# A transformer block on one core: early sums moved to GpSimd, loads and turnings placed anew, the last output behind the loop over other pairs

## The chip, the core and the metric

The kernel runs on one core of a Trainium2 chip. The core has TensorE (PE, matrix products into PSUM; its weight loads are listed apart as PEld), VectorE (DVE), ScalarE (ACT), GpSimd (POOL) and SyncE (SP). SP and ACT issue most of the DMAs, POOL the indirect ones. The metric is the time on the device in microseconds, of one execution of the whole program; lower is better.

## The reference

The input is x: 8 sequences of 512 rows of 256 numbers, all in fp32.

```
x = x + layernorm(attention(layernorm(x)))
x = x + layernorm(ffn(layernorm(x)))
```

The attention has 16 query heads of width 128 in 4 groups that share keys and values, a causal mask, biases and a sinusoidal position term added to queries and keys; an output product brings 2048 back to 256. The ffn routes each of the 4096 rows to 6 of 64 experts by a softmax. Each expert takes the first 64 rows that chose it, in row order, and no more: `d = (silu(rows @ w_gate) * (rows @ w_up)) @ w_down`, weighted by the score of the row. To their sum a shared expert of inner width 352 is added for every row.

## The kernel before, in words

The order of all instructions on the five engines is written out by hand: inside `tc.manual_schedule` each engine runs what the Python code records, in the order in which it records it. So the place of a call in the code is its place in each engine's queue, DMAs included.

The main loop (L998) runs over k = 0 to 127, one attention head of one sequence per round (b = k // 16, s = k % 16). A round is called a head, or a slot, below. Per head: `scores` (four triangular tiles psc, reduced on DVE to e and least, exponentiated on ACT), `weigh` (four scalings of e, on POOL, for the last head on DVE), `turned` (DVE transposes e in 32x32 blocks to eb, SP stores it to DRAM as ex_d and reads it back in turn as et), `mix` (et times values into pav, evicted by ACT as ao), `project` (ao times the output weights into po), `queries` (pq, evicted by DVE as qt). These belong to different heads: while head k is scored, head k - 1 is turned, k - 2 mixed, k - 3 projected. The last two heads are turned on TensorE instead (`turned_at_once`, L373), with evictions of the four tiles pe alternating between ACT and DVE.

Between these stand side tasks at named places of a head: A and B after `weigh` and `project`, M after `queries`, D at the end. They are the preparation of the next sequence (`prepare`: load of x, statistics, keys and values) and the feed-forward part of the previous one (`feed_forward`: residual sum, normalised rows xg, shared expert with products psg and psu, routing). For the first four sequences the turned rows xt go through DRAM too, as exr_d: four writes at the step "6M", and a read behind the next head's writes of ex_d.

The experts are served in two ways. After five sequences (EARLY = 5) the experts are computed in pairs of two, 32 pairs, by the generator `experts` (L662), advanced two or four times per head from head 94 on. One pair in its turn: `start_pair` gathers rows by an indirect DMA on POOL (gx), `turn_rows` turns them on TensorE (ptx, copied by DVE to gxt), `gate_up`, `gate_up_hidden`, `turn_hidden` (pth, ht), `down` (pd, dd), `scatter` (an indirect adding DMA to y_d). Weights are loaded on ACT's queue. An iteration of the generator has two halves. When all pairs are done, `finish_early` (L969) adds the two halves of y_d for the first five sequences, normalises and stores the output: one sequence starts every four half slots, each with `finish` (L699), which takes seven of them.

The last three sequences are served for one pair "late", which still has places free, with products inside `feed_forward` and `last_part` (L886). Further such pairs, if any, are served by a loop over other pairs (L1073), whose count is computed at run time. In the profiled execution no instruction of the loop's body is listed: the count is zero. `last_part` works through the feed-forward of sequence 7, with the shared expert and the output of sequence 6 in between.

PSUM pools ps_s (scores, turnings) and ps_m (products) have three buffers each. Before the first experts run, `zeros` (L228) clears the second half of y_d by 21 stores on SP; the main loop advances it twice per head in the first sequence.

## Time and profile before

| what | us |
|---|---|
| runs: median (lowest, highest) | 1431.27 (1430.13, 1436.82) |
| the profiled execution's own time | 1429.28 |
| its span, from the first to the last instruction | 1427.6 |
| TensorE busy | 1383.4 (97%) |
| VectorE, ScalarE, GpSimd busy | 895.4, 500.2, 433.7 |
| mean granted TensorE clock | 0.994 |
| DMA moved | 262.5 MB, mean 184 GB/s |

A row of the profile names a line of the kernel, an engine, an operation and the tiles that it writes and reads ("psc<-kt,qt"). Times are in microseconds unless marked ns. A wait names the instruction that ended it. "PEclk" is the share of TensorE's full clock that the chip granted. An engine that stands costs time only if the end of the program hangs on it.

### The profile page before, as it was taken

Reading aid. Unit: us, or ns where it says so; the run is one execution under the profiler, and the core shown is the slowest. Engines: PE = TensorE matmul, PEld = TensorE weight load, DVE = VectorE, ACT = ScalarE, POOL = GpSimd, SP = SyncE. Lnnn points to the kernel's source line nnn. Section 1 sums busy time; section 2 is a strip of 40 time slices with the busy share of each in tenths; the row PEclk is TensorE's granted clock in tenths of the full one; section 3 lists DMA queues with packets and bytes.
Section 4 is the critical chain, followed back from the end, with each engine's and each line's share of the span. In section 5 each row is a group of like instructions: output and inputs, shape, how many; then the busy total and the mean of one; then the engine's idle time right before and its main releaser. Section 6 shows DMA issues by size and latency. Waiting matters only on the chain.

```text
span 1427.6 us, 18526 instructions
## 1 busy us (share of the span) xinstructions
PE 1383.4 (97%) x5230; PEld 841.4 (59%) x5230; DVE 895.4 (63%) x3127; ACT 500.2 (35%) x1432; POOL 433.7 (30%) x698
## 2 busy tenths in 40 slices
PE   9999999999999999999999999999989999999895
PEld 5665665666556665656556665655546565556463
DVE  5565577656775577557765677566656545677634
ACT  2332344224332334234422433233433333444421
POOL 2222242213321242114221232124545344444311
PEclk9999999999999999999999999999999999999998
DMA  7774566546763576455654566459999889877702
GB/s 243 204 225 146 140 181 198 146 119 171 215 177 107 150 208 193 110 140 164 207 164 125 155 173 193 107 147 276 302 246 258 225 239 252 210 236 250 240 30 82
DMA packets 167990, 262.50 MB, mean 184 GB/s; under 512 B 17212, under 2 KB 142109, under 8 KB 167885
## 3 DMA queue, kind: packets, MB, share of 16 engines
q1 hardware_dynamic: 133069, 212.00, 50.5%
q10 hardware_dynamic: 28672, 39.85, 9.4%
q0 software_dynamic: 6144, 9.44, 3.4%
q8 instruction: 42, 0.69, 0.2%
q14 instruction: 63, 0.52, 0.1%
HBM read 148.25 MB, written 112.99 MB: 183 GB/s over the span
## 4 chain that ended last, share of the span: by engine, by line
PE 80%; DMA 7%; DVE 7%; issue 2%; ACT 2%; POOL 1%; SPq 1%; ACTq 0%; DVEq 0%; POOLq 0%
PE pav L390 16%; PE psc L328 15%; PE pq L315 13%; PE po L402 13%; PE pk L285 4%; PE pv L296 4%; PE psg L749 3%; PE psu L749 3%; PE pgu L590 2%; PE py L776 2%; PE pd L616 2%; DMA wd<-in_w_down 2%; DVE eb L361 1%; DMA exr_d<-xb_f 1%; ACT e L335 1%
## 5 line engine op out<-in xcount | busy, mean ns | idle before, releaser
L345 POOL TENSOR_SCALAR e<-e,recip 128x128 f32<-128x128 f32 x508 | 268.5, 574 | 757.6 <-DVE recip L342 744.0
L335 ACT ACTIVATE e<-e,least 128x128 f32<-128x128 f32 (+3 forms) x512 | 285.8, 559 | 349.2 <-DVE least L332 337.1
L328 PE MATMUL psc<-kt,qt 128*128 128x128 f32 (+3 forms) x1024 | 306.3, 438 | 8.6 <-DVE least L332 6.0
L390 PE MATMUL pav<-et,v 128*128 128x512 f32 (+3 forms) x1024 | 297.5, 434 | 3.3 <-DMA et<-ex_d 3.0
L390 PEld LDWEIGHTS pav<-et,v 128*128 128x128 f32 x1024 | 194.1, 190 | 165.7 <-issue 116.8
L332 DVE CUSTOM_DVE_ANT_0 e<-psc,mask 128x128 f32<-128x128 f32 (+3 forms) x512 | 232.6, 479 | 56.3 <-PE psc L328 49.4
L402 PE MATMUL po<-wo_sb,ao 128*128 128x256 f32 x1024 | 243.5, 381 | 0.7 <-ACT ao L110 0.7
L315 PE MATMUL pq<-xnt,wq_sb 128*128 128x512 f32 x512 | 242.2, 596 | 0.0
L402 PEld LDWEIGHTS po<-wo_sb,ao 128*128 128x128 f32 x1024 | 193.1, 190 | 72.0 <-issue 41.0
L110 ACT COPY ao<-pav 128x512 f32<-128x512 f32 x128 | 74.9, 585 | 443.8 <-PE pav L390 429.6
L361 DVE STREAM_TRANSPOSE eb<-e 128x128 f32<-128x128 f32 x756 | 227.4, 364 | 3.5 <-DMA ex_d<-eb 3.2
L328 PEld LDWEIGHTS psc<-kt,qt 128*128 128x128 f32 x1024 | 164.6, 191 | 76.7 <-DVE least L332 26.9
L318 DVE SCALAR_TENSOR_TENSOR qt<-pq,bq_sb,pe_sb 128x512 f32<-128x512 f32 x128 | 95.6, 747 | 104.6 <-PE pq L315 104.4
L315 PEld LDWEIGHTS pq<-xnt,wq_sb 128*128 128x128 f32 x512 | 96.3, 191 | 69.7 <-issue 64.3
L342 DVE RECIPROCAL recip<-total 128x4 f32<-128x4 f32 x128 | 22.8, 178 | 120.2 <-ACT e L335 120.2
L335 ACT ACTIVATION_READ_ACCUMULATOR e<-e,least 128x1 f32 x512 | 95.8, 187 | 0.0
L627 POOL DMA_INDIRECT y_d<-dd,idx x32 | 50.9, 1591 | 102.0 <-DMA y_d<-dd,idx 51.5
L285 PE MATMUL pk<-xnt,wkv_sb 128*128 128x512 f32 x128 | 59.3, 594 | 0.2 <-ACT xnt L110 0.2
L296 PE MATMUL pv<-wkv_sb,xnt 128*128 128x512 f32 x128 | 58.1, 593 | 0.0
L298 DVE TENSOR_TENSOR v<-pv,bv_sb 128x512 f32<-128x512 f32 x32 | 22.1, 691 | 49.7 <-PE pv L296 49.7
L288 DVE SCALAR_TENSOR_TENSOR kt<-pk,bk_sb,pe_sb 128x512 f32<-128x512 f32 x32 | 24.0, 750 | 44.1 <-PE pk L285 44.1
L113 DVE COPY ht<-pth 88x256 f32<-88x256 f32 x32 | 13.4, 418 | 56.6 <-PE pth L607 56.6
(200 smaller groups left out, 1100.0 us busy)
## 6 DMA issues: line engine op xcount, KB each, us to landing
ex_d<-eb SPq DMA_DIRECT2D x504, 160.0 KB
et<-ex_d SPq DMA_DIRECT2D x126, 640.0 KB
wgu<-in_w_gate ACTq DMA_DIRECT2D x32, 352.0 KB
wgu<-in_w_up ACTq DMA_DIRECT2D x32, 352.0 KB
wd<-in_w_down ACTq DMA_DIRECT2D x32, 352.0 KB
y<-y_d ACTq DMA_DIRECT2D x10, 512.0 KB
x<-in_x SPq DMA_DIRECT2D x8, 512.0 KB
x_d<-x SPq DMA_DIRECT2D x8, 512.0 KB
```

The costliest lines, as they stand in the source:

```text
L285: nc.tensor.matmul(pk, lhsT=wkv_sb[:, c, g, 0, :], rhs=s["xnt"][:, c, :], start=c == 0, stop=c == NC - 1)
L296: nc.tensor.matmul(pv, lhsT=s["xnt"][:, c, ts(i, P)], rhs=wkv_sb[:, c, :, 1, :], start=c == 0, stop=c == NC - 1)
L315: nc.tensor.matmul(pq, lhsT=wq_sb[h // QPG][:, c, ts(h % QPG, D)], rhs=seqs[b]["xnt"][:, c, :], start=c == 0, stop=c == NC - 1)
L318: nc.vector.scalar_tensor_tensor(qt, pq, bq_sb[:, h : h + 1], pe_sb, ALU.add, ALU.add)
L328: nc.tensor.matmul(psc[:, :w], lhsT=l["qt"][:, ts(i, P)], rhs=seqs[b]["kt"][h // QPG][:, :w], start=True, stop=True)
L332: nc.vector.tensor_tensor_reduce(out=e, in0=psc[:, :w], in1=mask[:, T - w :], scale=-1.0 / math.sqrt(D), scalar=BIG, op0=ALU.add, op1=ALU. ...
L335: nc.scalar.activation(e, e, AF.Exp, bias=l["least"][:, i : i + 1], scale=-1.0, accum_out=l["total"][:, i : i + 1])
L345: engine.tensor_scalar(e, e, recip[:, n : n + 1], 1.0, ALU.mult, ALU.mult)
L361: nc.vector.transpose(blocks.rearrange("p c j t -> p j c t"), l["e"][i][:, js[0] * P : (js[-1] + 1) * P].rearrange("p (j c t) -> p j c t", ...
L390: nc.tensor.matmul(pav[:, :, j:, :], lhsT=seqs[b]["v"][:, j, ts(g, D)], rhs=l["et"][:, :, AT[j] : AT[j] + NI - j, :], start=j == 0, stop=j ...
L402: nc.tensor.matmul(po[b][i // 2][:, i % 2, :], lhsT=ao[:, ts(i, P)], rhs=wo_sb[:, h, :], start=h == 0 and i % 2 == 0, stop=h == NH - 1, sk ...
L749: nc.tensor.matmul(as_taken(pp[:mw, :], xt2), lhsT=w_sb[:, c, ds(f0, mw)], rhs=in_order(xt2, c), start=c == 0, stop=c == NC - 1)
```

## The change

- `zeros` is advanced once per head, in heads 0 to 22, instead of twice per head in heads 0 to 15.
- The load of the next sequence's x (the first step of `prepare`, at s = 6) is issued after step M instead of ahead of `queries`.
- `turn_rows` moves from the first half of an iteration of `experts` to the end of the second half.
- The down weights of the late pair are loaded in head 104 instead of 102.
- `finish`: the sum of the two halves is made by GpSimd, one half slot later, with the load of x1 beside it and a half slot of nothing behind it; a sequence takes nine half slots, and the steps end two half slots later.
- `output`: shift is computed in two parts, a product with -1 on DVE and a product with rs on GpSimd, both ahead of the pause.
- The last two heads: the project of head 124 goes ahead of the turning of head 126, whose evictions all go to DVE; the eviction of the last pav is split between DVE and ACT.
- `last_part` no longer stores x1 and y of sequence 7, gives sequence 6's output earlier places, and ends with the late pair's dd. The rest, `last_output`, comes after the loop over other pairs. In the loop, sequence 7 adds its term directly to the sums in PSUM.

```diff
--- before.py
+++ after.py
@@ -370,7 +370,7 @@
             l["et"] = p2.tile([P, NI, NB, BS], F32, tag="et", name=f"et_{k}")
             nc.sync.dma_start(out=l["et"].rearrange("s a n t -> s (a n t)"), in_=ex.rearrange("p a f -> p (a f)"))
-        def turned_at_once(k):
+        def turned_at_once(k, evictions=(on_act, on_dve) * 2):
             l = live[k]
             l["et"] = p2.tile([P, NI, NB, BS], F32, tag="et", name=f"et_{k}")
@@ -378,8 +378,8 @@
                 pt = ps_s.tile([P, NI, NI, BS], F32, tag="s", name=f"pe_{k}_{j}")
                 for i in range(j, NI):
                     nc.tensor.transpose(pt[:, i - j, :, :].rearrange("p a t -> p (a t)"), l["e"][i][:, ts(j, P)], ident)
-                (on_act, on_dve)[j % 2](l["et"][:, :, AT[j] : AT[j] + NI - j, :].rearrange("p a n t -> p n a t"),
-                                        pt[:, : NI - j, :, :])
+                evictions[j](l["et"][:, :, AT[j] : AT[j] + NI - j, :].rearrange("p a n t -> p n a t"),
+                             pt[:, : NI - j, :, :])
         def mix(k):
             b, h = divmod(k, NH)
@@ -390,7 +390,12 @@
                 nc.tensor.matmul(pav[:, :, j:, :], lhsT=seqs[b]["v"][:, j, ts(g, D)],
                                  rhs=l["et"][:, :, AT[j] : AT[j] + NI - j, :], start=j == 0, stop=j == NI - 1)
             l["ao"] = p2.tile([D, T], F32, tag="ao", name=f"ao_{k}")
-            on_act(l["ao"].rearrange("d (i a t) -> d i a t", i=NI, a=NI), pav.rearrange("d a i t -> d i a t"))
+            ao, rows = l["ao"].rearrange("d (i a t) -> d i a t", i=NI, a=NI), pav.rearrange("d a i t -> d i a t")
+            if k < NK - 1:
+                on_act(ao, rows)
+            else:
+                on_dve(ao[:, :2], rows[:, :2])
+                on_act(ao[:, 2:], rows[:, 2:])
         def project(k):
             b, h = divmod(k, NH)
@@ -668,8 +673,7 @@
             for m in range(NM + 5):
                 if m < NM:
                     start_pair(m)
-                for behind_, step in ((5, down), (3, gate_up), (4, turn_hidden), (2, turn_rows),
-                                      (1, load_gate_up), (3, load_down)):
+                for behind_, step in ((5, down), (3, gate_up), (4, turn_hidden), (1, load_gate_up), (3, load_down)):
                     if 0 <= m - behind_ < NM:
                         step(m - behind_)
                 yield
@@ -677,6 +681,8 @@
                     gate_up_hidden(m - 3)
                 if 0 <= m - 5 < NM:
                     scatter(m - 5)
+                if 0 <= m - 2 < NM:
+                    turn_rows(m - 2)
                 if m >= 2:
                     next(later, None)
                 if m == NM + 4:
@@ -686,8 +692,10 @@
         def output(b, y, x1):
             mv, rs = norm_scales(tiles_of(y), f"y{b}")
-            yield
-            shift = shifts(mv, rs, f"y{b}")
+            shift = small.tile([P, NI], F32, tag="shift", name=f"shift_y{b}")
+            nc.vector.tensor_scalar_mul(shift, mv[:, :, 0], -1.0)
+            nc.gpsimd.tensor_tensor(shift, shift, rs, ALU.mult)
+            yield
             for i in range(NI):
                 scale_on_act(y[:, i, :], y[:, i, :], rs, shift, i)
             for i in range(NI):
@@ -702,9 +710,11 @@
             for k in range(2):
                 nc.scalar.dma_start(out=ys[k], in_=rows_of(y_d, k * (ET_ROWS + CAP) + b * T))
             yield
+            yield
+            yield
             x1 = residual(b, *tags[2])
-            yield
-            nc.vector.tensor_add(ys[0], ys[0], ys[1])
+            nc.gpsimd.tensor_add(ys[0], ys[0], ys[1])
+            yield
             yield
             for n, _ in enumerate(output(b, ys[0], x1)):
                 yield
@@ -918,7 +928,6 @@
             transpose_rows(xt2, xg, f"f{b}")
             for i in range(NI):
                 nc.gpsimd.tensor_scalar(xt[:, i, :], xt[:, i, :], shift[:, i : i + 1], 1.0, ALU.add, ALU.mult)
-            nc.sync.dma_start(out=rows_of(x1_d, b * T), in_=xt)
             other["part"](py6, 0)
             f = shared(b, xt2, l, "msmsms")
             next(f)
@@ -937,32 +946,33 @@
             gather("late", [(xg, marked[0])])
             gt = turn_scores(marked[1], b, p2, "kt", 5)
             gate_up("late")
-            next(f)
+            output6()
             py = l["py"] = [ps_o.tile([P, 2, E], F32, tag=f"o{n}", name=f"py_{b}_{n}") for n in range(2)]
             l["part"](py, 2)
             l["part"](py, 1)
             gate_up_hidden("late")
+            next(f)
+            output6()
             turn_hidden("late")
             l["part"](py, 0)
+            output6()
             down("late")
-            output6()
-            output6()
-            output6()
-            for i in range(NI):
-                nc.tensor.matmul(py[i // 2][:, i % 2, :], lhsT=gt[:, ts(i, P)], rhs=pairs["late"]["dd"],
-                                 start=False, stop=True, skip_group_check=True)
+            return py, xt, gt, pairs["late"]["dd"]
+
+        def last_output(py, x1, gt, dd):
+            b = B - 1
+            for i in range(NI):
+                nc.tensor.matmul(py[i // 2][:, i % 2, :], lhsT=gt[:, ts(i, P)], rhs=dd, start=False, stop=True,
+                                 skip_group_check=True)
             mv, rs = norm_scales([py[i // 2][:, i % 2, :] for i in range(NI)], f"y{b}")
             y = p2.tile([P, NI, E], F32, tag="xnt", name=f"y_{b}")
-            for n in range(2):
-                nc.scalar.copy(y[:, ts(n, 2), :], py[n])
-            nc.sync.dma_start(out=rows_of(ly_d, b * T - ET_ROWS), in_=y)
-            for i in range(NI):
-                nc.vector.tensor_scalar(o[:, i, :], py[i // 2][:, i % 2, :], mv[:, i, 0:1], None, ALU.subtract)
-            for i in range(NI):
-                nc.vector.scalar_tensor_tensor(xt[:, i, :], o[:, i, :], rs[:, i : i + 1], xt[:, i, :],
-                                               ALU.mult, ALU.add)
+            for i in range(NI):
+                nc.vector.tensor_scalar(y[:, i, :], py[i // 2][:, i % 2, :], mv[:, i, 0:1], None, ALU.subtract)
+            for i in range(NI):
+                nc.vector.scalar_tensor_tensor(x1[:, i, :], y[:, i, :], rs[:, i : i + 1], x1[:, i, :], ALU.mult, ALU.add)
                 if i % 2:
-                    nc.sync.dma_start(out=rows_of(out, b * T)[:, i - 1 : i + 1, :], in_=xt[:, i - 1 : i + 1, :])
+                    nc.sync.dma_start(out=rows_of(out, b * T)[:, i - 1 : i + 1, :], in_=x1[:, i - 1 : i + 1, :])
+
         EARLY_TAGS = [(p3, "wgu"), (p3, "wd")]
@@ -970,9 +980,9 @@
             rows = [finish(b, EARLY_TAGS + [[(p1, "xn"), (p2, "xnt")][b % 2]]) for b in range(EARLY)]
             yield
-            for t in range(4 * EARLY + 3):
+            for t in range(4 * EARLY + 5):
                 for b in range(EARLY):
-                    if 0 <= t - 4 * b < 7:
+                    if 0 <= t - 4 * b < 9:
                         next(rows[b])
                 yield
@@ -1007,32 +1017,32 @@
             scores(k, 2)
             scores(k, 3)
             if k == NK - 1:
-                turned_at_once(k - 1)
+                project(k - 3)
+                turned_at_once(k - 1, (on_dve,) * NI)
             weigh(k)
             side(s, "A")
-            if k >= 3:
+            if 3 <= k < NK - 1:
                 project(k - 3)
             side(s, "B")
             if active and not finishing:
                 next(routed, None)
             if s == 9 and b <= EARLY + 1:
                 next(ahead)()
-            if s == 6 and b <= EARLY:
-                ahead = prepare(b + 1)
-                next(ahead)()
             if k + 1 < NK:
                 queries(k + 1)
             if finishing:
                 next(routed, None)
             side(s, "M")
+            if s == 6 and b <= EARLY:
+                ahead = prepare(b + 1)
+                next(ahead)()
             if b <= EARLY and s == 8:
                 next(ahead)()
             if k >= 2:
                 mix(k - 2)
             if active and not finishing:
                 next(routed, None)
-            if not b:
-                next(zeroing, None)
+            if k < NH + 7:
                 next(zeroing, None)
             if k == FIRST_FREE:
@@ -1042,6 +1052,7 @@
                 pairs["late"] = {"m": table["m"], "wgu_at": {"tag": "wgu_late", "bufs": 1},
                                  "wd_at": {"tag": "wd_late", "bufs": 1}}
                 load_gate_up("late")
+            if k == FIRST_FREE + 2:
                 load_down("late")
             if s == 2 and b:
                 behind = feed_forward(b - 1)
@@ -1065,7 +1076,7 @@
         turned_at_once(NK - 1)
         mix(NK - 1)
         project(NK - 1)
-        last_part(behind, routed)
+        sums, *last = last_part(behind, routed)
         order.close()
@@ -1080,7 +1091,7 @@
                 q, tag = [(p1, "hid"), (p2, "v"), (p2, "v")][b - EARLY]
                 xg = q.tile([P, NI, LROW], F32, tag=tag, name=f"rest_xg_{b}")
                 nc.sync.dma_start(out=xg, in_=rows_of(lxg_d, b * T - ET_ROWS))
-                q, tag = [(p1, "y"), (p2, "x"), (p2, "x")][b - EARLY]
+                q, tag = [(p1, "y"), (p2, "x"), (p1, "xt2")][b - EARLY]
                 mark, marked = marks(m, xg[:, :, E:ROW], xg[:, :, ROW:], f"rest_{b}", q, tag)
                 parts.append((xg, mark))
                 gts.append(turn_scores(marked, f"rest_{b}", p2, "kt", 5))
@@ -1089,7 +1100,10 @@
             gate_up_hidden("late")
             turn_hidden("late")
             down("late")
-            for b in range(EARLY, B):
+            for i in range(NI):
+                nc.tensor.matmul(sums[i // 2][:, i % 2, :], lhsT=gts[-1][:, ts(i, P)], rhs=pairs["late"]["dd"],
+                                 start=False, stop=False, skip_group_check=True)
+            for b in range(EARLY, B - 1):
                 y = p2.tile([P, NI, E], F32, tag="xnt", name=f"rest_y_{b}")
                 nc.sync.dma_start(out=y, in_=rows_of(ly_d, b * T - ET_ROWS))
                 for i in range(NI):
@@ -1099,6 +1113,8 @@
                 nc.sync.dma_start(out=rows_of(ly_d, b * T - ET_ROWS), in_=y)
                 for _ in output(b, y, residual(b, p1, "xn")):
                     pass
+        with tc.manual_schedule(engines={ET.PE, ET.DVE, ET.Activation, ET.Pool, ET.SP}):
+            last_output(sums, *last)
 # ---- launch: one core ----
```

## The prediction

> **What bounds the kernel now.** I read the page first, for the engine that is never free; then the waits of that engine; then the stages where it waits.
>
> ```profile
> PE 1383.4 (97%) x5230; PEld 841.4 (59%) x5230; DVE 895.4 (63%) x3127; ACT 500.2 (35%) x1432; POOL 433.7 (30%) x698
> ```
>
> TensorE is busy for 1383.4 of 1427.6 us, and the change takes no TensorE instruction from the work. It can win only among the 44.2 us in which TensorE stands: 15.4 after its last matmul (1412.2), 1.9 ahead of its first, and some 27 of waits. Its waits by releaser:
>
> ```profile
> PE psc L328 <- DVE least L332: 6.0, 6, 2.4
> PE psg L749 <- DMA xt<-exr_d: 4.7, 4, 1.5
> PE pav L390 <- DMA et<-ex_d: 3.0, 3, 2.3
> PE pd L616 <- DMA wd<-in_w_down: 2.9, 2, 2.1
> PE ptx L579 <- DMA gx<-xg_d,idx: 2.3, 1, 2.3
> PE pe L380 <- ACT et L110: 2.2, 1, 2.2
> ```
>
> Total, times, longest: no wait repeats in every head; each is one collision at one place, and nearly each of these places is touched by the change. Two of them cost more than they say. TensorE by time around the first turning of gathered rows (start, duration, in brackets the standing before):
>
> ```profile
> 964.88 0.48 PE L579 MATMUL ptx<-ident,gx 128*128 128x128 f32 x2 [2.27 <-DMA gx<-xg_d,idx]
> 965.19 3.25 PE L315 MATMUL pq<-xnt,wq_sb 128*128 128x512 f32 x4
> ```
>
> The stretches of 10 us around it and around the wait for wd (length; busy time of PE, PEld, DVE, ACT, POOL; granted clock; DMA share; GB/s):
>
> ```profile
> 960.00:970.00 10.00, 7.73 (x21) 4.02 (x20) 4.83 (x19) 2.31 (x8) 4.98 (x7) 0.83 0.95 330
> 970.00:980.00 10.00, 10.00 (x50) 5.80 (x49) 5.79 (x24) 4.51 (x13) 1.31 (x3) 1.00 0.77 224
> ...
> 1050.00:1060.00 10.00, 7.63 (x31) 3.94 (x29) 5.01 (x18) 3.85 (x15) 1.50 (x2) 0.83 0.98 270
> ```
>
> After the 2.27 us of standing the clock is 0.83 and four query matmuls take 3.25 us, elsewhere 1.88.
>
> **Early stage: zero stores and the x load.** One store of zeros a head instead of two, over 22 heads instead of 11. The row is the wait for et (2.3 at 109.9 us, 0.25 at 86): its read was issued at 106.3 behind two stores of 128 KB and landed about 112.6. One of them gone, at some 200 GB/s, is 0.65 us, and 0.5 of SP issue; the same holds for the head before. I take 2.0 of 2.55 (0 to 2.5). The longer tail of stores ends in head 21, ahead of the exchange in head 22.
>
> The x load of the next sequence moves behind step M, so behind the four exchange writes on SP:
>
> ```profile
> 215.07 0.40 SPq L167 DMA_DIRECT2D x<-in_x  x1
> 215.56 2.48 SPq L133 DMA_DIRECT2D exr_d<-xb_f  x4
> 218.09 2.80 SPq L366 DMA_DIRECT2D ex_d<-eb  x4
> 222.13 0.34 SPq L135 DMA_DIRECT2D xt<-exr_d  x1
> ```
>
> The read at 222.13 waited for the writes, which ran behind 512 KB of x, and the last ex_d write waited for the x load's landing (220.59). Without both the read goes out 1 to 2 us earlier, and each of the four psg waits is 0.9 to 1.5 us: 3.5 of 4.7 (0 to 4.7). What is late instead is x, which is not read until the next head.
>
> **Expert stage.** Turning the gathered rows moves half an iteration later, past the step M or D and POOL's scatter. The first wait, 2.3 us, falls away: the rows came at 964.9, and the new place, behind the mix, is about 968. [...]
>
> The turning also held PSUM: psc's second tile waited for the copy of ht in the buffer before it, 0.2 us (start to start 0.33 where 0.11 is usual, at 1124.24) in 15 of these heads. In the changed order two score tiles and the turning lie apart: 15 x 0.2 = 3.0; new small waits for least eat some. I take 2.5 (0 to 3.3). start_pair on POOL now waits for a turning issued just ahead of it; behind it is only a scatter, half a head before the next scaling of e, so nothing.
>
> The late pair's down weights load two heads later. They were issued at 1030.6 among eight weight loads with the DMA engines at 0.98 to 1.06, and pd then stood 2.9 us for wd, with 1.25 of slow clock (0.83 above; the gate and up products at 1054.6 took 0.55 a step where 0.29 is usual). 352 KB at 290 GB/s is 1.2 us off that queue: 2.0 (0 to 4.1), since the other loads stay. They are read five heads later.
>
> **Finishing stage: the early sums.** DVE loses five adds of 1.225 us; POOL gets five of 128x1024 and five small products. POOL shows adds of 128x256:
>
> ```profile
> L694 POOL TENSOR_TENSOR x<-x,y x28: 720/728/737, 1171.7 to 1413.4; 128x256 f32<-128x256 f32 x28
> 1323.98 1.23 DVE L707 TENSOR_TENSOR y<-y,y 128x1024 f32<-128x1024 f32 x1 [5.11 <-DMA ex_d<-eb]
> ```
>
> Four of them back to back take 2.77 us, so a sum some 2.8. It starts when the head's four scalings of e (2.05 us) end, and the next head's start 7 to 9 us later: hidden, and behind it wait only those scalings. DVE no longer stands 5.1 us for y's load with scores behind it, nor 2.2 for rs_y. After 1250 the psc waits for least are 5.2 us: 0.67 is in the last head; I win back 0.5 of the 0.5 at 1262, 0.6 of the 1.3 at 1292 (y's statistics there move beside another routing step, 2.0 + 1.2 us of DVE instead of 3.7), 2.2 of 2.4 at 1323, 0.3 of the rest, 0.4 of a wait for gt: 4.0 (0 to 5). The y loads have half a head more to land; the x1 load, 512 KB on SP, moves a head later with the sums and is read a head and a half after it.
>
> [...]
>
> **Last two heads.** The project of head 124 goes ahead of the turning, whose four evictions go to DVE: the 2.2 us wait and 0.67 of least end. But the fifth sequence's scaling (four ACTIVATEs, 2.1 us) now stands on ACT ahead of the eviction of head 126. Counted from the last head's first score: DVE's weigh ends at 8.0, statistics 9.9, rs and product 11.3, ACT 13.5, eviction 14.1, where TensorE wants it at 12.2: 1.9 lost; mix of head 125 waits 0.5 for its et. Splitting the last eviction: 0.58 to about 0.35. Together +0.6 (-1 to +2.5).
>
> In the last part, sequence 6's statistics (2.0 us of DVE) come ahead of the hidden product of the late pair, which is 0.2 later and not wanted by TensorE until 1406.4: nothing. The last sequence's two stores of 512 KB and two copies on ACT (1.04 us) are gone; nothing waited for them but the queue below.
>
> **The end.** The last dd products wait until the loop over other pairs is passed.
>
> ```profile
> 1416.04 1.63 SPq L965 DMA_DIRECT2D out_dram<-x  x2
> L1148 POOLq DRAIN  x3: 46/103/5303, 1421.4 to 1427.3; - x3
> ```
>
> Before: products at 1410.2, last x at 1416.8, stores landed 1421.0, all engines met there, POOL drained for 5.3 us, end 1427.6. After: sequence 6's output goes earlier, its store at about 1408.5, landed 1411.4 (a lone 512 KB store took 2.9, at 1382.9). The engines meet at about 1411.8 and the products start at 1412.0, +1.8. Then 6.6 to the last x, 2.5 for stores that no longer queue behind 1 MB: 1421.1. POOL is free after its power, 1416.5; if the drain runs from there it ends 1421.8, and with the last 0.8 the end is 1422.6: 5.0 gained. If it starts only after the stores: 1427.2, 0.4. A fetch of code after the jump (TensorE's first branch showed 1.9 us) could make it -1.5. Nearer the first: 4.0 (-1.5 to 5).
>
> **Sum.** 2.0 + 3.5 + 4.0 + 2.5 + 2.0 + 4.0 + 0.6 + 4.0 = 22.6 us, from the profiled execution's 1429.28: 1406.7. That execution lies 2.0 under the median 1431.27, so 1408.7: 1409.
>
> **Rivals.** (a) Likeliest, as summed: 1409, own range 1401 to 1416 (all ends taken would be 31). Chance 0.55. (b) The transfers' waits only move: zeros, x, wd and the tail gain nothing, 11.1 stay: 1420. For it: the DMA share is 0.9 to 1.0 from 980 to 1060, and a late load on ACT's queue can hold a write on SP's (in the chain of waits ex_d at 1322.0 follows the landing of y). Against: at the early places the share is 0.63 to 0.87. 0.27. (c) The change doesn't do what it says: TensorE pulled ahead meets the next late tile, as in the last head here: 1428, within 0.5% (7 us; a measurement of this kernel tells no less). 0.10. (d) Slower: gate_up after the turning. In half of the pairs (16) only down lies between, 1.08 us of cover for the copy gxt, whose 0.42 us start 0.4 after the turning. If DVE is behind, TensorE stands each time; it decides from 1.4 us beyond the cover (16 x 1.4 eats the gain), and at 2.5 (40 us), with the gains kept, the time is 1449. DVE is half idle there, so 0.08.
>
> Faster 0.82, same 0.10, slower 0.08. Range 1400 to 1425: it leaves out (c) and (d).
>
> **What will show.** Right: no wait of ptx and no 0.83 near 960; psg waits under 0.3; no least wait over 1 after 1250; POOL sums of about 2.8 with scalings on time; a wait of 2 us for ao in the last head; last matmul about 10 us from the end. Wrong: gxt as a releaser of pgu, e late on POOL, or a drain that starts after the last store.

## The result, and the profile after

The changed kernel takes 1423.44 us (median of 8 runs, 1420.27 to 1427.39), the kernel before 1431.44 beside it: a ratio of 0.995 (95% interval 0.9935 to 0.9966). In a second set of runs it was 1424.78 against 1429.69, ratio 0.9965 (0.9951 to 0.998). So the change gains 5 to 8 us. Forecast were 22.6. (Ratios here and below are to the kernel before, run on the same chip; between runs the ratios compare better than the times.) One of the 14 executions of e3_finish_old took 4536 us at the full granted clock, for a reason that stays open; the ratios leave it out.

TensorE's busy time is what it was. First the page of the changed kernel, then its waits by releaser (total, times, longest):

```profile
PE 1381.9 (97%) x5230; PEld 839.9 (59%) x5230; DVE 887.4 (62%) x3125; ACT 497.5 (35%) x1428; POOL 446.1 (31%) x710
```

```profile
PE psc L328 <- DVE least L332: 10.9, 7, 2.5
PE pav L390 <- DMA et<-ex_d: 5.5, 4, 1.9
PE py L965 <- SPq L1084: 2.9, 1, 2.9
...
PE po L407 <- ACT ao L110: 1.8, 1, 1.8
PE ptx L584 <- DVE ht L113: 1.7, 1, 1.7
...
PE psg L759 <- DMA xt<-exr_d: 0.2, 1, 0.2
```

Gone are the waits for gathered rows (2.3), for wd (2.9), for the exchanged rows (4.7, now 0.2) and for ScalarE's et (2.2). But psc waits for least 10.9 in place of 6.0, pav for et 5.5 in place of 3.0, psc for qt 2.0 and pt_f for xg 1.9 in place of 0.8 each, and three waits are new: at the loop, for ao at 1360, for ht. Added up, the two lists give 27.2 us of waits before and 30.8 after. What was taken away stands somewhere else; what this execution gained lies behind TensorE's last matmul, 15.4 us before and 8.6 after (1413.5 to 1422.0).

To see where, I take the start of each head's first score product and compare stretches. One trace is one execution, and some waits in it are chance; so the table uses all traces of this study whose code is the same in that stretch (mean, and how many traces), and the forecast beside it. The rows up to head 16 and from head 73 to 99 take either place of the x load as the same. The trace of e2_xstats is left out (with it, heads 99 to 111 would be 206.3 and heads 111 to 127 173.1).

| stretch | forecast | before | changed | difference |
|---|---|---|---|---|
| start to head 16 (zeros) | -2.0 | 160.1 (3) | 157.8 (14) | -2.3 |
| heads 16 to 73 (x load) | -3.5 | 543.0 (3) | 547.0 (9) | +4.0 |
| heads 73 to 99 (first turning) | -4.0 | 267.9 (3) | 265.2 (13) | -2.7 |
| heads 99 to 111 (turning, wd) | -4.5 | 207.7 (3) | 206.4 (10) | -1.3 |
| heads 111 to 127 (early sums) | -4.0 | 169.8 (3) | 172.8 (8) | +3.0 |
| head 127 to the end | -4.6 | 78.6 (2) | 73.7 (9) | -5.0 |
| sum | -22.6 | | | -4.3 |

Single traces spread by 4 to 7 us in three rows (heads 16 to 73 of the changed kernel 545.2 to 552.2, heads 111 to 127 169.7 to 175.4). Three rows came as forecast, within 1.3; three are off by 7.5, 3.2 and 7.0. The rows that came right show in the profile as they should. The turning near 960 has no wait for rows, and the stretch of 10 us around it keeps its clock (length; busy PE, PEld, DVE, ACT, POOL; granted clock; DMA share; GB/s):

```profile
960.00:970.00 10.00, 9.48 (x41) 5.92 (x39) 5.65 (x23) 4.56 (x12) 5.61 (x9) 1.00 0.91 306
```

At the end, the last products start at 1410.2, as before, but now behind the loop; the stores are issued at 1417, and GpSimd's drain (the instruction with which its queue ends) begins at 1414.8, with its last power (1414.84 to 1415.86), not behind the stores:

```profile
1410.21 1.14 PE L965 MATMUL py<-dd_late,gt 128*128 128x256 f32 x3 [2.95 <-SPq L1084]
```

```profile
1417.14 1.16 SPq L974 DMA_DIRECT2D out_dram<-x  x2
```

```profile
L1164 POOLq DRAIN  x3: 46/109/6382, 1414.8 to 1421.8; - x3
```

The drain is listed with 6.4 us, of which the power takes the first 1.0; it ends at 1421.2, and the span ends at 1422.0.

### The profile page after: what moved, and what is told of

Same layout as the page of the kernel before. It is cut to its first block, busy times and chain, and to the rows that moved or that the text cites. A ratio compares the mean times of both kernels' runs of the same rounds, so it can differ in the third digit from the quotient of the medians.

```text
span 1422.0 us, 18479 instructions
## 1 busy us (share of the span) xinstructions
PE 1381.9 (97%) x5230; PEld 839.9 (59%) x5230; DVE 887.4 (62%) x3125; ACT 497.5 (35%) x1428; POOL 446.1 (31%) x710
## 5 line engine op out<-in xcount | busy, mean ns | idle before, releaser
L328 PE MATMUL psc<-kt,qt 128*128 128x128 f32 (+3 forms) x1024 | 304.8, 436 | 12.9 <-DVE least L332 10.9
L407 PEld LDWEIGHTS po<-wo_sb,ao 128*128 128x128 f32 x1024 | 193.0, 190 | 74.5 <-issue 41.7
L595 PE MATMUL pgu<-wgu,gxt 128*64 128x352 f32 x256 | 43.6, 461 | 0.7 <-issue 0.7
```

The source lines that it names most:

```text
L328: nc.tensor.matmul(psc[:, :w], lhsT=l["qt"][:, ts(i, P)], rhs=seqs[b]["kt"][h // QPG][:, :w], start=True, stop=True)
L407: nc.tensor.matmul(po[b][i // 2][:, i % 2, :], lhsT=ao[:, ts(i, P)], rhs=wo_sb[:, h, :], start=h == 0 and i % 2 == 0, stop=h == NH - 1, sk ...
```

## The experiments

### 1. The load of x

In the changed kernel the wait of psg is gone (0.2), but not because its rows come earlier. SP's queue and VectorE around the first exchange (times from the start; in brackets the standing before):

```profile
214.29 1.83 SPq L133 DMA_DIRECT2D exr_d<-xb_f  x4
216.16 0.46 SPq L167 DMA_DIRECT2D x<-in_x  x1
216.67 2.90 SPq L366 DMA_DIRECT2D ex_d<-eb  x4
220.00 0.34 SPq L135 DMA_DIRECT2D xt<-exr_d  x1
```

```profile
221.85 1.41 DVE L78 BATCH_NORM_STATS2 st_a<-x 128x6 f32<-128x256 f32 x4 [1.99 <-DMA x<-in_x]
223.18 0.36 DVE L84 BATCH_NORM_AGGREGATE mv_a<-st_a 128x2 f32<-128x6 f32 x4
```

```profile
224.00 1.12 PE L328 MATMUL psc<-kt,qt 128*128 128x512 f32 x2 [1.46 <-DVE least L332]
224.96 1.88 PE L759 MATMUL psg<-xt,sg_sb 128*128 128x512 f32 x4
```

The statistics of x stand on VectorE's queue ahead of the next head's score reductions. They now wait 1.99 us for x, the reductions wait behind them, TensorE waits for the reductions, and by the time it has come through that wait and one more score product the exchanged rows are there (the last of the read's completions is at 224.71). TensorE's wait is 1.5 to 2.1 us at each of the four exchanges. The rows themselves are later than before: counted from the head's start, the read of xt went out after 6.6 to 6.9 us in place of 7.4 to 8.0, and its last completion came after 11.6 to 12.3 in place of 11.1 to 11.6. Undoing the move alone (e1_xload_old):

```diff
+            if s == 6 and b <= EARLY:
+                ahead = prepare(b + 1)
+                next(ahead)()
             if k + 1 < NK:
                 queries(k + 1)
...
             side(s, "M")
-            if s == 6 and b <= EARLY:
-                ahead = prepare(b + 1)
-                next(ahead)()
```

> The changed kernel with the load of x back at its place ahead of the queries, nothing else undone. Theory (the move of the load lost 2.7 us in the stretch of heads 16 to 73, by statistics that wait for x): that stretch takes 443.5 us in place of 446.3, with four waits of psg of 0.9 to 1.5 us again and none of psc for least over 0.3 there: 1420.7, from 1419.5 to 1422. Rival (the loss there comes of something else, the longer tail of zero stores or the order of the exchange): 446 us for the stretch and 1423.

Measured: 1420.35 us, ratio 0.9941 (0.9919 to 0.9962); heads 16 to 73 took 543.7 (the changed kernel in nine traces 545.2 to 552.2), and the four psg waits were back at 0.7 to 1.7. As the theory said (this expectation and that of e8_x_behind write the stretch 100 us too short: 443.5 stands for 543.5); the four later traces with x at its old place gave 542.6 to 543.7. Next, leave x late and take its statistics out of the way (e2_xstats: they move to step M of head 8, the normalisation to step D):

```diff
-                           (0, 0, 0, 0, 0, 0, 0, 1, 0, 0, 1, 1, 2, 1, 2, 2)[s]):
+                           (0, 0, 0, 0, 0, 0, 0, 0, 1, 0, 1, 1, 2, 1, 2, 2)[s]):
```

> The changed kernel, with the statistics of the next sequence's x put half a head and more later on VectorE (step M of head s = 8 in place of step D of head s = 7); the load of x stays at its late place. Theory (the late x holds the statistics, and these hold the next head's score reductions on VectorE): the four waits of psc for least of 1.6, 1.9, 1.8 and 2.3 us at 222, 379, 535 and 692 fall under 0.3, the wait of psg for xt stays at 0.2 in all, and the head starts in the middle of the program come 6 us earlier than in the changed kernel (2.7 that its move of the load lost, and the 3.5 that the prediction wanted from it): 1417.2, from 1416 to 1419. Rival (the DMA engines are what is short, and the loss only moves to the normalisation, the exchange of x or a read of et): 1421 to 1424, with a new wait of like size within two heads.

Measured: 1442.66 us, ratio 1.0102 (1.0072 to 1.0132). My theory was wrong in its second half, and this run told most. The waits for least at 222 went, and TensorE came to psg 2 us earlier, only to wait there:

```profile
219.02 0.53 SPq L167 DMA_DIRECT2D x<-in_x  x1
219.59 2.77 SPq L366 DMA_DIRECT2D ex_d<-eb  x4
222.52 0.40 SPq L135 DMA_DIRECT2D xt<-exr_d  x1
```

```profile
227.93 1.96 PE L759 MATMUL psg<-xt,sg_sb 128*128 128x512 f32 x4 [1.85 <-DMA xt<-exr_d]
```

The read of xt is issued 6.8 us after its head's start (before the change 8.0), but its rows arrive 5.4 us later, where before the change they took 3.8 (222.13 to 225.95). What the read gains at its issue it loses under way, with x's 512 KB beside it: from the head's start to psg 12.2 us against 11.8. The four psg waits are 7.1 in all, more than the 4.7 before. Besides, the normalisation at its new place made a new wait for least of 1.9 us in each sequence, with slow matmuls behind it. In all this trace is 21.6 us longer than the changed kernel's, with 6.9 more of psg waits, 5.0 more of waits for least, and seven more slow stretches of 1.7 us each. So x has to be out of the exchange altogether (e8_x_behind: load behind the read of xt, statistics ahead of the queries of head 8, normalisation where it was):

```diff
-            if s == 9 and b <= EARLY + 1:
+            if s == 7 and b <= EARLY:
+                ahead = prepare(b + 1)
+            if s in (7, 8) and b <= EARLY or s == 9 and b <= EARLY + 1:
                 next(ahead)()
...
             side(s, "M")
-            if s == 6 and b <= EARLY:
-                ahead = prepare(b + 1)
-                next(ahead)()
...
-                           (0, 0, 0, 0, 0, 0, 0, 1, 0, 0, 1, 1, 2, 1, 2, 2)[s]):
+                           (0, 0, 0, 0, 0, 0, 0, 0, 0, 0, 1, 1, 2, 1, 2, 2)[s]):
```

> The changed kernel, with the load of the next sequence's x issued only behind the read of the exchanged rows xt (head s = 7), and its statistics ahead of the queries of head s = 8. Theory (512 KB of x share the DMA engines with the exchange, ahead of the four writes before the change and beside the read after it, so that the change of place could not bring the rows earlier: the read went out 1.1 us earlier and travelled 1.6 us longer): with x out of the way altogether, psg finds its rows, no statistics wait for x, the waits of psc for least at 222, 379, 535 and 692 fall under 0.3 and those of psg for xt stay under 0.3 each; the stretch of heads 16 to 73 takes 440.5 to 443 us in place of 446.3 (before 443.5) and the time is 1417.5, from 1416 to 1420. Rival (the exchange itself, eight writes and a read behind them, takes that long): psg waits 0.8 to 1.6 us in each of the four places as before the change, 443 to 445 us for the stretch, 1420 to 1422.

Measured: 1423.3 us, ratio 0.9957 (0.9937 to 0.9976), heads 16 to 73 542.9.

```profile
220.17 0.34 SPq L135 DMA_DIRECT2D xt<-exr_d  x1
221.79 0.34 SPq L371 DMA_DIRECT2D et<-ex_d  x1
222.17 0.44 SPq L167 DMA_DIRECT2D x<-in_x  x1
```

The psg waits fell from 4.7 to 1.4 us in all (three of at most 0.6), so x beside the exchange was most of them. But the statistics cost a wait for least of 0.4 at their new place, and in the sixth sequence, where there is no exchange, one of 2.2 us with slow matmuls behind it (heads 73 to 99: 269.5 in place of 265.2). It gained 0.4 in the stretch against the place of before (542.9 against 543.3 in the five traces with x there) and lost 4.2 behind it. No place tried for x beats the old one.

### 2. The early sums

Undone as a whole in the changed kernel (e3_finish_old), and made alone in the kernel before (e6_finish_alone); the diff of both is the part on `finish`, `output` and `finish_early` shown with the change.

> The changed kernel, with the early sums, their output steps and their timing as they were before the change (sums on VectorE, y loads half a head ahead of the x1 load). Theory (the finishing steps in their new form cost what the stretch from 1181 to 1349 lost, 4.7 us): 1418.7, from 1417.5 to 1420; waits for et after 1250 gone, the wait for least at 1289 back to about 1.3. Rival one (the stretch lost because TensorE came into it 6 us earlier and met transfers and POOL steps that did not come earlier): 1422 to 1424 with the waits for qt at 1247 and for et still there. Rival two (the prediction's own sum: the sums on GpSimd gain 4.0): 1427.

> The kernel before, with only the early sums, the output steps and their timing taken from the change. Theory one (the new finishing steps cost by themselves): heads 111 to 127 take 171.5 to 173.5 us in place of 168.6, with waits for et of 1.5 to 2 us, and the time is 1434, from 1432.5 to 1436. Theory two (putting the finishing steps back in the changed kernel won only 2.8 of 4.7 us: part of the loss is the meeting of an earlier TensorE with transfers that are no earlier): 169.5 to 171 us, 1431.5 to 1433. Rival (the prediction's sum for this part): 164.6 us, 1427.

Measured: e3_finish_old 1422.62 us, ratio 0.9963 (0.9944 to 0.9982), and heads 111 to 127 in 170.6. e6_finish_alone 1425.05, ratio 0.9969 (0.9953 to 0.9985), and 171.4. In the stretch both say that the new finishing steps lose: 170.6 without them and 173.3 and 175.1 with, 171.4 with them and 168.6 and 170.3 without. Theory and time still disagree: undone they gave back nothing that can be told from the changed kernel's time, and alone they made the kernel faster. For the second, the trace has a reason in part: with sums and outputs later, the fifth sequence's four scalings on ScalarE (2.08 us at 1351.7 in the kernel before) no longer stand in front of the exponentials and the eviction behind them for which the turning of the last head but one waited 2.2 us (now 0.2), and from head 127 to the end it took 74.8 us in place of 77.8 and 79.5. The finishing steps lose about 2 us in their own stretch and win about 4 at the end, where I had credited the other parts of the change. Those do as much without them: in e3_finish_old the end takes 74.5. Both together give 73.7, so the two gains overlap. The rest of the 4.4 us by which e6_finish_alone is faster lies, in its one trace, ahead of head 111, where its code is that of before, and stays open.

What they lose in the stretch has one clear piece. VectorE and GpSimd of the changed kernel at a routing step:

```profile
1288.05 0.32 DVE L443 TENSOR_SCALAR xg<-sc,grecip 128x64 f32<-128x64 f32 x1
1288.40 0.23 DVE L444 MAX8 top<-xg 128x8 f32<-128x64 f32 x1
1288.55 2.13 DVE L443 TENSOR_SCALAR xg<-sc,grecip 128x64 f32<-128x64 f32 x1
1290.86 0.24 DVE L443 TENSOR_SCALAR xg<-sc,grecip 128x64 f32<-128x64 f32 x1
```

```profile
1288.29 2.34 POOL L716 TENSOR_TENSOR y<-y,y 128x1024 f32<-128x1024 f32 x1
```

The sum on GpSimd ends at 1290.63. A product of 128x64 on VectorE, 0.24 us when nothing runs beside it, starts at 1288.55 and ends with the sum. TensorE then waits 2.5 us for least, where it was 1.3. MAX8 in between takes its usual 0.23. It is so in every one of the 14 traces with whole sums on GpSimd: 2.5 us each time. Sums back on VectorE, all else as changed (e4_sum_dve):

```diff
-            nc.gpsimd.tensor_add(ys[0], ys[0], ys[1])
+            nc.vector.tensor_add(ys[0], ys[0], ys[1])
```

> The changed kernel, with only the five sums put back on VectorE at the same late place; loads, store and all other steps as changed. Theory one (a sum on GpSimd blocks a VectorE instruction, seen as a TENSOR_SCALAR of 2.13 us in place of 0.3 at 1288.6, while the waits for et come from four 512 KB transfers that are issued together): the 2.5 us wait for least at 1289 becomes 1.3 or less, five adds of 1.2 us come back on VectorE and cost up to 2 of it again, the waits for et of 1.9 and 1.6 stay: 1422 to 1425. Theory two (the sum on GpSimd is all that the finishing steps lost): 1418.7 to 1420, and the waits for et go too.

Measured: 1422.64 us, ratio 0.9955 (0.994 to 0.9971); the wait near 1288 is 1.3, heads 119 to 122 take 28.85 us, as in the kernel before (28.90), in place of 30.1 or 31.7. The waits for et stay (2.6 and 1.0). Theory one. I then moved the sums half a head later (e13_sum_later: a pause of the generator ahead of the sum in place of behind it).

> The changed kernel with only the five sums on GpSimd half a head later. Theory (one sum meets the routing step on VectorE, and that is the whole loss from GpSimd's sums): the wait of psc for least near 1288 falls from 2.5 to about 1.3 or less, no VectorE instruction beside a sum takes over twice its usual time, the waits for et at 1325 and 1344 stay: heads 111 to 127 take 171 to 172 us in place of 173.3 and 175.1; 1422. Rival (wherever it stands, a sum of 2.3 us meets something on VectorE): a TENSOR_SCALAR or TENSOR_TENSOR of VectorE stretched by over 1 us beside at least one sum, 173 to 175 us, 1424.

Measured: 1422.75 us, ratio 0.9962 (0.9939 to 0.9985), the wait 2.5 as ever. The edit had moved nothing: between the two places no other instruction goes to GpSimd, so in its queue the sum stood where it had stood. It tested neither theory, and serves as one more trace of the changed kernel. What does test it is a cut: four adds of 128x256 in place of one (e14_sum_split, on the kernel of six repairs below).

```diff
-            nc.gpsimd.tensor_add(ys[0], ys[0], ys[1])
+            for i in range(NI):
+                nc.gpsimd.tensor_add(ys[0][:, i, :], ys[0][:, i, :], ys[1][:, i, :])
```

> The kernel of six repairs with each of the five sums on GpSimd cut into four adds of 128x256. Theory (a VectorE instruction waits for the end of the one GpSimd instruction that runs): no TENSOR_SCALAR of that routing step takes over 0.8 us where one took 2.13, the wait of psc for least near 1284 falls from 2.5 to under 1.7, heads 119 to 122 take 30.5 us or less in place of 31.7, and the time falls by 1 to 2 us: 1414. Rival (VectorE waits until GpSimd has nothing ready, or the four adds together, 2.8 us, hold it in turns): the routing step as a whole is as late, wait 2.3 to 3 us, time as without the cut, 1415.6.

Measured: 1411.94 us, ratio 0.9871 (0.9826 to 0.9915). VectorE and GpSimd of this run at the same step:

```profile
1282.07 0.52 DVE L443 TENSOR_SCALAR xg<-sc,grecip 128x64 f32<-128x64 f32 x1
1282.62 0.23 DVE L444 MAX8 top<-xg 128x8 f32<-128x64 f32 x1
1282.76 0.50 DVE L443 TENSOR_SCALAR xg<-sc,grecip 128x64 f32<-128x64 f32 x1
```

```profile
1281.80 2.77 POOL L717 TENSOR_TENSOR y<-y,y 128x256 f32<-128x256 f32 x4
```

The same work on GpSimd, 2.8 us in place of 2.3, but the product waits for the end of one add and not of all: 0.52 in place of 2.13. TensorE's wait is 1.4, heads 119 to 122 take 29.0. That settles what this wait hangs on, the length of the one instruction that GpSimd runs; the time alone would not, since the same kernel with whole sums, run beside it, has 0.9878 (e11_again, below). What these traces show is this one product: 2.13 us beside the whole sum, 0.50 and 0.52 beside the cut one, 0.24 alone. By what GpSimd holds it, no trace shows.

The other piece is the y loads. Waits of SP's queue between 1240 and 1360, first before, then changed:

```profile
SPq L366 <- DMA y<-y_d: 4.5, 1, 4.5
...
SPq L371 <- DMA y<-y_d: 1.8, 1, 1.8
```

```profile
SPq L366 <- DMA y<-y_d: 10.4, 5, 5.3
```

Writes of ex_d wait for the landing of y loads that were issued on another queue, now in all five sequences, and behind the writes stands the read of et that TensorE wants. Before the change the late y held the sum on VectorE, and so least (2.4 us at 1323); in the changed kernel it holds a write, and so et (1.9 at 1325 and 1.6 at 1344): the write that SP holds until a y load has landed goes out at 1318.97, the read of et behind it at 1323.28, and pav starts at 1327.40. The waits come with the finishing steps: 4.0 for y and at most 0.4 for et in e3_finish_old, 12.0 for y, 1.8 and 1.7 for et in e6_finish_alone. That the y loads alone make et late is argued from these times; no run freed the writes. Two tries to loosen this. In e5_spread the store and the x1 load were laid apart from the y loads:

> The changed kernel, with the sums on GpSimd as changed, but the transfers of the finishing steps laid apart: the two y loads in one half head, the store of an earlier output a half head later, the x1 load another half head later. In the changed kernel these four transfers of 512 KB are issued within a few us, and five writes of ex_d wait 10.4 us in all for y. Theory (the transfers issued together make the writes and then the read of et late): the waits for y on SP fall under 5, the waits for et at 1325 and 1344 (1.9 and 1.6) go, and the time is 1419.5, from 1418.5 to 1421; the 2.5 us for least at 1289 stays. Rival (the bytes have to go anyway, or the sum on GpSimd is the cause): 1423, within 1 us.

Measured: 1428.17 us, ratio 0.9993 (0.9973 to 1.0012), heads 111 to 127 175.6. It failed: the x1 load now came right behind the store of the output that leaves the same buffer, and SP stood for it.

```profile
SPq L727 <- DMA out_dram<-x: 15.2, 3, 5.1
```

In e7_y_apart only the second y load is issued half a head later:

```diff
             for k in range(2):
                 nc.scalar.dma_start(out=ys[k], in_=rows_of(y_d, k * (ET_ROWS + CAP) + b * T))
-            yield
-            yield
+                yield
             yield
```

> The changed kernel with the second y load of each early sequence issued half a head after the first; all else as changed. Theory (two y loads of 512 KB are issued together beside an x1 load and a store, and writes of ex_d on SP wait for their landing, then the read of et, then TensorE): the five waits of ex_d for y (10.4 us in all) fall under 5, the waits for et at 1325 and 1344 (1.9 and 1.6 us) fall under 0.5 each, and the stretch of heads 111 to 127 takes 169.5 to 171 us in place of 173.3: 1420.5. Rival (the bytes of the stretch are too many for the engines wherever they are put, or another write is caught in place of these): 172.5 to 174 us, 1423.

Measured: 1423.91 us, ratio 0.9955 (0.9938 to 0.9972); heads 111 to 127 170.0, the waits for et 0.5 and 1.1. But SP's waits for y stayed at 10.4, which the theory had under 5, and in four later traces with this edit the waits for et were 0.4 to 1.8. It helps a little (171.2 on average over the four traces that have it with whole sums, 172.8 without), not for the reason that I gave; how much of it is real stays open.

### 3. Turning and weights, heads 73 to 111

The turning back in the first half (e9_turn_old):

> The changed kernel with the turning of gathered rows back in the first half of an iteration, all else as changed. Theory (the late place saves the wait for the first gathered rows and the slow matmuls behind it, and little else): heads 73 to 99 take 268 to 269.5 us in place of 265.2, with a wait of ptx for gx of about 2 us near 960 and a granted clock under 0.9 in those 10 us; heads 99 to 111 take 205 to 209 as before; the 1.3 to 3.3 us wait of ptx for ht near 1058 goes, waits of psc for ht of 0.2 us come back in some 15 heads: 1425 to 1427. Rival one (the prediction's sum, 4.0 and 2.5): 1430. Rival two (the wait for ht that the late place brings eats what it gains): 1421 to 1423.

Measured: 1423.33 us, ratio 0.9971 (0.9955 to 0.9986). Heads 73 to 99 took 269.6 in place of 265.2, with a wait of 2.6 us for rows at 962; heads 106 to 111 97.3 in place of 96.5, the small waits for ht. But heads 99 to 111 as a whole took 204.3, less than nearly all traces with the late turning. Rival two: the late turning gains at the first pair and pays near 1058. VectorE there, in the changed kernel, and TensorE:

```profile
1059.24 1.39 DVE L78 BATCH_NORM_STATS2 st_a<-x 128x6 f32<-128x256 f32 x4
1060.54 0.36 DVE L84 BATCH_NORM_AGGREGATE mv_a<-st_a 128x2 f32<-128x6 f32 x4
1060.94 0.17 DVE L86 TENSOR_SCALAR ve_a<-mv_a 128x4 f32<-128x4 f32 x1
1061.02 0.41 DVE L113 COPY ht<-pth 88x256 f32<-88x256 f32 x1
```

```profile
1061.49 0.50 PE L584 MATMUL ptx<-ident,gx 128*128 128x128 f32 x2 [1.65 <-DVE ht L113]
```

The turning needs the PSUM buffer that the copy of ht frees, and that copy stands behind a routing step and the statistics of x on VectorE. At its old place the turning followed the copy at a distance. The wait was 1.3 to 3.3 us in all twelve traces with this order, 2.3 on average. The load of the late pair's down weights put back alone (e12_wd_old):

```diff
-            if k == FIRST_FREE + 2:
                 load_down("late")
```

> The changed kernel with the late pair's down weights loaded in head 102 again. Theory (the two heads later keep 352 KB from the weights that are wanted): a wait of pd for wd of 1 to 3 us between 1010 and 1055 comes back, and heads 99 to 111 take 208 to 210 us in place of 205.0 and 206.1: 1426. Rival (the wait for wd is one that comes and goes from run to run): no such wait over 0.8, 205 to 207 us, 1423 to 1425.

Measured: 1425.42 us, ratio 0.9981 (0.9963 to 0.9998); 207.2 us for heads 99 to 111, with a wait for wd of 0.6 and one of 2.1 of the queries for ScalarE's routing at 1053. Neither theory: the wait for wd came back, but small. The kernel before had 2.1 there in one trace and 0.6 in the other. What the late load is worth stays open, between nothing and 2 us.

### 4. Single traces against each other

Both kernels once more (before_again, after_again):

> The kernel before as it is, once more, for the same reason. By the first trace: 156.1 within 0.3 for each sequence of 16 heads from 25 to 73, 269.2 for heads 73 to 99, 208.6 for heads 99 to 111, 168.6 for heads 111 to 127, 77.8 from head 127 to the end. Theory (what the change gained and lost is of the program): these hold within 1 us, but for heads 99 to 111. Rival (single waits in it, as the 2.3 us for gathered rows at 965, the 2.4 us for least at 1323 and the 2.2 us for et at 1354, are chance of one execution): some of these stages come out 2 to 4 us shorter. Time 1428 to 1432.

> The changed kernel as it is, once more, to see which of the differences between single traces are of the program and which of one execution. If a stage's time is the program's own, it repeats: 157.0 within 0.3 for each sequence of 16 heads from 25 to 73, 265.2 for heads 73 to 99, 73.5 from head 127 to the end. For heads 99 to 111, where the other runs with the same code there gave 204.6 to 208.9 (205.0 in the first trace), I expect a value between 205 and 209; for heads 111 to 127, 172 to 174. Time 1421 to 1425.

Measured: 1427.49 (ratio 0.9995, 0.9977 to 1.0013) and 1424.78 us. The stages repeat within 1.8 us, not within the 1 us expected; heads 73 to 99 of the changed kernel repeat to 0.01. The losses of 4.0 and 3.0, over many traces, are larger than that and so the program's. But one row on which the prediction stood did not repeat. The first turning of the kernel before, second trace:

```profile
964.96 0.48 PE L579 MATMUL ptx<-ident,gx 128*128 128x128 f32 x2 [2.37 <-DMA gx<-xg_d,idx]
965.28 1.88 PE L315 MATMUL pq<-xnt,wq_sb 128*128 128x512 f32 x4
```

It waits 2.37 us, longer than the 2.27 of the first trace, and no slow matmul follows. The clock records of the two traces tell why. In both, the clock goes by stretches of 3.41 us that are either whole or half; first before, then before_again, laid on these stretches (columns as above; the first busy time is TensorE's, the last but two the clock):

```profile
962.14:965.55 3.41, 1.14 (x6) 0.60 (x5) 0.84 (x4) 1.41 (x4) 1.68 (x4) 1.00 1.02 338
965.55:968.97 3.42, 3.42 (x5) 1.33 (x4) 0.89 (x3) 0.00 (x0) 2.34 (x3) 0.50 1.02 367
```

```profile
960.26:963.67 3.41, 2.33 (x10) 1.52 (x8) 2.47 (x10) 2.03 (x8) 0.73 (x1) 1.00 0.98 306
963.67:967.09 3.42, 2.13 (x7) 1.21 (x8) 0.57 (x3) 0.00 (x0) 3.07 (x5) 1.00 1.03 348
```

In the first trace the whole standing falls into one stretch, of which TensorE is idle for 2.27 us, and the next runs at half clock. In the second it lies across two, 1.08 and 1.29 us, and neither is followed by a slow one.

### 5. The repairs together

e10_best puts x back, issues the second y load later, evicts head 126's product on VectorE (ScalarE had four scalings of the fifth output ahead of it) and takes the statistics of sequence 6's output ahead of the late pair's gather. The third of these repairs answers this in the changed kernel, ScalarE and TensorE:

```profile
1359.36 2.08 ACT L98 ACTIVATE y<-y,shift_y,rs_y 128x256 f32<-128x256 f32 x4 [2.37 <-POOL shift_y L697]
1361.34 0.56 ACT L110 COPY ao<-pav 128x512 f32<-128x512 f32 x1
```

```profile
1361.96 1.99 PE L407 MATMUL po<-wo_sb,ao 128*128 128x256 f32 x8 [1.76 <-ACT ao L110]
```

```diff
             if k < NK - 1:
-                on_act(ao, rows)
+                (on_act if k < NK - 2 else on_dve)(ao, rows)
...
             next(f)
             next(f)
+            output6()
             gather("late", [(xg, marked[0])])
             gt = turn_scores(marked[1], b, p2, "kt", 5)
             gate_up("late")
-            output6()
```

> The changed kernel with four repairs at places where the runs so far showed a loss: the load of x back ahead of the queries (2.7 us in the stretch of heads 16 to 73), the second y load of each early sequence half a head later (3.4 us in heads 111 to 127), the eviction of the product of head 126 on VectorE in place of ScalarE, where four scalings of the fifth sequence's output stand ahead of it (wait of po for ao of 1.8 us at 1360), and the statistics of sequence 6's output ahead of the gather of the late pair, so that its store, on which the engines wait at the loop, goes out 1.3 us earlier. Theory (each of these losses is a thing of its own place): 1423.4 - 2.7 - 3.4 - 1.7 - 1.3 = 1414.3, from 1412 to 1418; ratio to the kernel before 0.988. Rival (TensorE that comes earlier meets the next late tile, so that repairs at different places do not add): 1419 to 1421, with new waits of 1 to 3 us behind the repaired places.

Measured: 1419.61 us (4 runs, 1415.11 to 1420.81), ratio 0.9939 (0.9922 to 0.9955). In its trace the stretches did what was expected of them (543.7; 170.3; from head 127 to the end 71.5 in place of 73.7, with no wait for ao and 2.1 at the loop in place of 2.9), and no new wait over 1 us stood behind a repaired place, so the repairs add in the trace. But that execution was the fastest of the four (1415.11); the median lay 5 us above the sum, at the rival's figure. Two more repairs (e11_stats_sum: the sum's half head, which moved nothing, and the statistics of the last sequence's x a head earlier), and a repeat of them beside the cut sums (e11_again):

```diff
-            for _ in range((0, 0, 0, 0, 0, 0, 1, 0, 1, 1, 2, 1, 1, 1, 2, 1)[s] if b == EARLY + 1 else 0 if b > EARLY else
+            for _ in range((0, 0, 0, 0, 0, 0, 1, 1, 0, 1, 2, 1, 1, 1, 2, 1)[s] if b == EARLY + 1 else 0 if b > EARLY else
```

> The kernel with four repairs of the run before, with two more: the statistics of the last sequence's x at step D of its head s = 7 in place of s = 8, and the five sums on GpSimd half a head later. Theory (the copy of ht stands behind 2 us of statistics and a routing step on VectorE's queue at about 1055; the sum on GpSimd holds a routing step at about 1282): the wait of ptx for ht falls from 2.9 to under 1 and heads 99 to 111 take 203 to 205 us in place of 206.5; the wait for least near 1282 falls from 2.5 to 1.3 or less and heads 111 to 127 take 168 to 169.5 in place of 170.3: 1415.5, from 1413 to 1418. Rival (other steps are caught): 206 and 170 to 172, 1419 to 1421.

> The kernel of six repairs once more, beside the cut sums. If its gain is its own, the ratio to the kernel before is 0.990 within 0.003 again, about 1414 to 1417 us; if it was a lucky hour of one chip, 0.994.

Measured: 1415.59 us, ratio 0.99 (0.9869 to 0.9931), and 1413.56, 0.9878 (0.9829 to 0.9927). The wait of ptx for ht was 1.6, none, and 1.2 in the three traces with the earlier statistics; heads 99 to 111 took 204.4 on average in place of 206.4. So, by three traces, the statistics were about 1.4 of the 2.3 us that this wait was on average; the routing step stands ahead of what is left. With the sums cut (e14_sum_split) the kernel takes 1411.94 us, ratio 0.9871: it beats both kernels (the changed one has 0.995 and 0.9965). The share of the cut in that cannot be told from the noise.

## Why the prediction was right or wrong

The predicted 1409 missed by 14 us; the range, 1400 to 1425, holds 1423.4 and holds 1424.8 barely. The direction was right. Of the cases, (b) with 1420 and (c) with 1428 lie about as near as each other. Case (b) had half of its terms right: the load of x gained nothing and the late weights little, but zeros and the tail gained, and the sums, which it left as gains, lost. What (c) says, that TensorE meets the next late tile, is what became of the exchange and of the turning near 1058. That the range holds the result is in part luck, since gains and losses that it had not foreseen in their places balanced.

- **Zeros, 2.0: right**, 2.3 over all traces. (The wait for et that it read at 109.9 stood from 110.5.)
- **The x load, 3.5: wrong by 7.5.** Two steps failed. "What is late instead is x, which is not read until the next head": its time was not worked out. The statistics are the last step of that head on VectorE, ahead of the next score reductions; VectorE came to them 3.7 us after the load's issue, and x was there after 5.7 (216.16 to 221.85). And "Without both the read goes out 1 to 2 us earlier": it went out 0.7 to 1.1 earlier, and its rows landed 0 to 1.0 later. With x behind the read (e8_x_behind) they landed 10.3 to 10.8 us after the head's start: 512 KB moved from ahead of a transfer to beside it still hold it up. The argument followed issues; what counted was the landing.
- **The first turning, 4.0: right in kind, 2.7 on average.** No run shows the 4.0, which takes 2.3 of standing and 1.7 of slow matmuls from one row; over all traces the stretch became 2.7 shorter. The wait itself (2.3) is saved for good. The 1.7 of slow matmuls behind it was not: it hung on where the standing lay against the 3.41 us stretches of the clock, which another execution did not repeat. I took one row for the mean.
- **ht and wd, 4.5: 1.3.** "new small waits for least eat some" looked for the wrong wait. The small waits did go (0.8 of the 2.5, in heads 106 to 111), but the late turning took over the buffer's wait in one place, 1.3 to 3.3 us. wd is open, between nothing and its 2.0.
- **The sums, 4.0: -3.0, wrong by 7.0.** Two terms. The 4.0 counts nothing for VectorE's standing beside a sum, and that standing cost 2.3 (heads 119 to 122 31.2 on average over 14 traces, 28.9 without). What was held was the routing step's product (2.13 us in place of 0.24), a place that I had not lined up with the sum. And "2.2 of 2.4 at 1323" was counted as won back, while the same y loads, through writes on SP, made et late by 1.9, as far as the times show. The prediction had read in the chain of waits that an ex_d write follows the landing of y, and used it only as a point for rival (b).
- **Last two heads and end, 4.6: right**, 5.0. The wait of 1.9 for ao was 1.76, the drain ran from the end of GpSimd's power as taken, the store of sequence 6 landed at 1409.2 (1411.4 forecast, the engines met 1.8 earlier). But the 2.2 us of et would have gone with the finishing steps alone. And the 1.9 read as TensorE's first branch was no cost of a jump: it is the time of TensorE's own last products (1410.2 to 1412.2), for which the next step waited; the branches themselves are listed with 0.10 to 0.30 us.

The sum of the misses, 7.5 + 1.3 + 3.2 + 7.0 less 0.7 for the two rows that came better, is 18.3 of 22.6.

## What to carry to other kernels

When a transfer or a step is moved, work out the time at which its data are wanted next, in the queue of the engine that reads them, and follow the bytes to their landing; an earlier issue beside the same bytes was no gain here (12.2 us from the head's start to psg in e2_xstats, 11.8 before). A stall that is taken from TensorE can uncover the next late tile (the waits were 27.2 us before, 30.8 after): count as won only what is left after naming that tile. An instruction moved to GpSimd should be short, since a VectorE instruction can stand until it ends (2.13 us here, beside a sum of 2.34); cutting that sum into four cost 0.4 us there and gave back 1.1, or 2.7 where a slow stretch of the clock had followed the wait.

## What the runs showed of the hardware

**How a standing of TensorE slows it.** The same wait of 2.52 us for least, in 14 traces, was followed by full speed in 5 and by 1.7 us of slow matmuls in 9. The 4 us behind it, first the changed kernel, then its second trace (columns as above, the eighth is the granted clock):

```profile
1293.00:1297.00 4.00, 4.00 (x15) 2.60 (x14) 2.65 (x10) 1.43 (x4) 0.73 (x2) 1.00 1.05 370
```

```profile
1292.00:1296.00 4.00, 4.00 (x12) 2.62 (x11) 2.47 (x10) 1.60 (x6) 0.55 (x2) 0.68 1.07 365
```

What decides between the two stands in the clock records. In all 19 traces TensorE's clock is either whole or half, the slow stretches are one or two times 3.413 us long (those at the start and at the end of the program apart), and within a trace they begin whole multiples of 3.413 us apart. So each execution has its own grid of windows. Where TensorE, by its listed matmuls, was idle for 1.96 us or more of a window at full clock, the next window ran at half clock, 54 times of 54; from 1.3 to 1.96 us 14 times of 92, for which no more is known; below 1.3 us never in some 7,500 windows. (The 1.96 is read from these same traces.) It is not the length of the standing alone that counts, but how much of it falls into one window. The 14 waits of 2.52 us follow this without exception: the 9 slow ones have 2.34 us or more in one window, the 5 others at most 1.84.

A slow window costs half of 3.41, 1.7 us, if TensorE has work for all of it: behind the wait the two groups psc and po took 2.07 and 2.63 us in after_again, 1.12 and 1.89 in the changed kernel's first trace. A wait of 2.5 us is so worth 2.5 + 9/14 x 1.7 = 3.6 us on average, and no single trace tells it. As an estimate from the 1.96 and the 3.41, a wait of 2.52 that begins anywhere in a window is followed by a slow one with a chance of 0.6, and the 2.27 us of the first turning with 0.5: it was worth about 3.1 us, less than the prediction's 4.0.

**GpSimd's drain at the end** ends 5.33 us after GpSimd's last piece of work in all 16 traces with the changed end, beside stores and VectorE's work. In the kernel before it begins behind the loop, at 1421.4, and takes 5.3 from there. It sets the end of the changed kernel: it ends at 1421.2, and the last store has landed at 1420.1.
